# Linear attention: keys times x first, the values' weights applied to that sum

## The chip, the cores and the metric

The kernel runs on one core of a Trainium2 chip. The metric is the device time of a whole execution in microseconds. One execution was also recorded by the hardware profiler; all durations of single instructions come from that execution.

## The reference, cut to what matters

The program is a chain of four layers on x of 2 images, 512 channels and 32 x 32 = 1024 pixels: layer 0 attention with a learned position bias and an MLP, layer 1 a deformable convolution with a gate, layer 2 linear attention, layer 3 softmax attention with 8 heads. The change lies in layer 2:

```python
def delu(x):
    return 10.0 * relu(x) + exp(10.0 * minimum(x, 0.0))
Q = einsum('dc,bcn->bdn', wq, xf) + bq[None, :, None]      # d = 64, c = 512, n = 1024
K = einsum('dc,bcn->bdn', wk, xf) + bk[None, :, None]
V = einsum('ec,bcn->ben', wv, xf) + bv[None, :, None]      # e = 512
Qf = delu(Q).transpose(0, 2, 1)
Kf = delu(K)
KV = einsum('bmn,bcn->bmc', Kf, V)
norm = 1.0 / einsum('bnd,bd->bn', Qf, sum(Kf, axis=-1) + EPS)
attn = einsum('bnd,bdc,bn->bcn', Qf, KV, norm)
return x + gamma[0] * attn
```

KV can be had in two orders. With V made first, it is Kf times V. With Kf times x made first, it is that 64 x 512 sum times wv, plus the sum of Kf over the pixels times bv.

## The kernel before, in words

All data is fp32. x lies in SBUF as `x_all`, with channels on partitions in four blocks (`CC` = 4) and pixels along the free dimension; each layer updates it in place. TensorE executes in exactly the order of the program text (a manual schedule). The instructions of the other engines are ordered by a planner, which mixes the streams of work on each of them; every engine then runs its own list in order. Layers are interleaved by Python generators: a `yield` in one lets the caller advance another.

Layer 1's deformable convolution has three parts for each image. `Products.run` makes, for each of 9 taps k, a table in DRAM: 8 pixel blocks of 128, each of four 128x512 matmuls `py` (L1281), copied by ScalarE to `y` (L1289, four buffers) and written by a DMA on SP's queue. `Samples.gather` fetches rows of that table by indirect DMAs that GpSimd issues (L1333), two for each block, 16 for each tap. `Samples.due` lets a tap's gathers start only when its table is complete. `Samples.add` accumulates what was gathered on VectorE (`dfacc`, L1344). `gate_image` ends the layer for one image.

Layer 2, `Linear.run`, is executed once per image:

- `pqk` (L1430): queries and keys of one half of the pixels in one 128-row result, queries in rows 0 to 63 and keys in rows 64 to 127; VectorE and ScalarE apply `delu`.
- In eight steps t, one per block of 128 pixels: `pv` (L1455), four 128x512 matmuls for the values, which VectorE evicts with the bias to `v` (L1463). At t=1 the keys are transposed (`pk`, L1468) and copied to `kf`. At t=3 the sum of the keys is made (`pks`, L1477). From then on each step also adds kf times v to `pkv` (L1448). At t=5 and t=6 the norms `pn` of the two halves follow (L1494), a reciprocal, and the scaling of the queries.
- `pkv` is copied to `kv` (L1509), and eight matmuls `pa` (L1514) with 64 rows apply it to the queries; VectorE adds each to x (L1522).

For image 0 this runs between the `py` matmuls of image 1's tables, one step of layer 2 for each block of a table, while image 1's gathers are under way. Then come layer 3's normalization `h` (L1612) and its queries and keys (`pq`, L1652) for image 0, with `gate_image` of image 1 among the last of these. For image 1, layer 2 runs together with layer 3's values of image 0 (`Attention.values`, L1629): `weave` takes one matmul of the values after each step of layer 2, and the rest of them (14) at the end. After that layer 3's heads start with scores `pl` (L1719), their maximum on VectorE (L1807), exponentials on ScalarE and transposes `pt` (L1769).

PSUM banks: layer 2 takes its results from a ring of five banks (`bank`) and one bank of its own for `pkv`; tables and values take a ring of two (`turn`).

Of the kernel before, what the change touches and what calls it, by code (L numbers as in the profile page):

```python
# [9 lines left out]
F32 = mybir.dt.float32  # L10
# [96 lines left out]
def layouts(i):  # L107
# [21 lines left out]
    for r in (0, 32, 64, 96):  # L129
        off_b[r : r + 18, 0] = np.asarray(i["L1_conv_off_b"])  # L130
    parts.append(("off_b", off_b))
    parts.append(("bqk", np.concatenate([i["L2_conv_bq"], i["L2_conv_bk"]]).reshape(128, 1)))
    parts.append(("gamma", _column(i["L2_conv_gamma"])))
    for name in ("gn_scale", "gn_bias", "b_out"):
        parts.append((name, _per_partition(i["L3_conv_" + name])))
# [18 lines left out]
    for g in range(8):  # L154
        vw_stack[64 * (g % 2) : 64 * (g % 2) + 64, g // 2] = vw[g].T

    off_w = np.asarray(i["L1_conv_off_w"]).reshape(18, CC, 128, 9).transpose(2, 1, 3, 0)
    dc_w = np.asarray(i["L1_conv_dc_w"]).reshape(C, CC, 128, 9).transpose(2, 3, 1, 0)
    qkv = np.asarray(i["L3_conv_W_qkv"]).reshape(C, 8, 3, 64)
    arrays = {  # L160
        "x": np.asarray(i["x"]).reshape(B, C, HW),
# [13 lines left out]
        "a_pw_w": _rows(np.asarray(i["L1_conv_a_pw_w"]).reshape(C, 256).T),  # L175
        "off_w": off_w,
        "dc_w": dc_w,
        "wqk": _rows(np.concatenate([i["L2_conv_wq"], i["L2_conv_wk"]]).T),
        "wv": _rows(np.asarray(i["L2_conv_wv"]).T),
        "dc_b_row": np.asarray(i["L1_conv_dc_b"]).reshape(1, C),  # L180
        "bv_row": np.asarray(i["L2_conv_bv"]).reshape(1, C),
# [94 lines left out]
def layers(net, out):  # L276
# [11 lines left out]
    with ExitStack() as later:  # L288
# [57 lines left out]
        with ExitStack() as l1:  # L346

            ps_m = net.psum(l1, "l1_m", 5)
            kv_bank = net.bank(l1, "l2_kv")
            banks["turn"] = net.psum(l1, "l1_y", 2)  # L350

            def bank(name):
                return ps_m.tile([128, 512], F32, name=name, tag="bank")

            att = Attention(net, later)
            l2 = ExitStack()
            linear = Linear(net, l2)
            own1 = ExitStack()
            f1 = Features(net, 1, own1)
            more = net.pool(own1, "df_more", 2)  # L360
            sums0.pools += [more, more]
            found = f1.run(bank, True)
            for i, _ in enumerate(made):
                some(found, 2)
                if i % 4 < 3:
                    sums0.due(taken)
            some(found, 99)
            sums1 = Samples(net, f1, products, own1, 1)
            sums1.pools += [more, more]
            tmp = net.pool(own1, "df_tmp", 1)  # L370
            made = products.run(f1, turn)
            taken1 = sums1.run()
            aside = None
            for i, _ in enumerate(made):
                if i == 62:
                    sums1.pools = sums1.pools[:3]
                if aside is None:
                    if next(taken, None) is None:
                        aside = gate_image(net, f0, sums0, tmp, bank)
                        wait = i + 4  # L380
                else:
                    sums1.due(taken1)
                    if i >= wait and next(aside, None) == "gated":
                        own0.close()
                        ctx2 = ExitStack()
                        extra = net.pool(ctx2, "df_extra", 2, side="right")
                        sums1.pools += [extra, extra]
                        linear.open(ctx2, side="right")
                        aside = chain(
                            linear.run(0, bank, kv_bank),  # L390
                            group_norm_terms(net, linear.tmp, 0, bank),
                        )
            for _ in aside:
                next(taken1, None)
            ctx2.close()
            image0.close()

            att.open_first(later, side="right")
            for _ in att.normalize(0):
                next(taken1, None)  # L400
            keys = chain(*(att.queries_keys(0, hp, turn) for hp in range(CC)))
            for i in range(48):
                next(keys)
                if i % 2 == 0:
                    next(taken1, None)
            some(taken1, 99)
            weave(keys, gate_image(net, f1, sums1, tmp, bank))
            own1.close()
            with ExitStack() as ctx:
                att.open_values(later, side="right")  # L410
                linear.open(ctx)
                weave(linear.run(1, bank, kv_bank), att.values(0, turn))
            l2.close()
        layer3(net, att, later, out)

# [2 lines left out]

FOUND = (1, 0, 0, 1, 2, 2, 2, 2, 0, 1, 1, 0, 3, 3, 3)
MADE = 11  # L420


def first_layer(net, pool, feat, p, q):
# [983 lines left out]
class Linear:  # L1407


    def __init__(self, net, ctx, **kw):  # L1410
        self.net, nc = net, net.nc
        w = net.pool(ctx, "l2_w", **kw)
        self.wqk, self.wv = net.load("wqk", w), net.load("wv", w)
        self.bv = net.load_row("bv_row", w)
        self.ones = w.tile([128, 64], F32, name="ones2", tag="ones2")
        nc.gpsimd.memset(self.ones, 1.0)
# [4 lines left out]
    def run(self, b, bank, kv_bank):  # L1421

        net, nc, x, tmp = self.net, self.net.nc, self.net.x, self.tmp
        qk = []
        for n in range(2):
            pqk = bank("pqk")
            for cc in range(CC):
                nc.tensor.matmul(  # L1430
                    pqk,
                    lhsT=self.wqk[:, cc, :],
                    rhs=x[:, b, cc, half(n)],
                    start=(cc == 0),
                    stop=(cc == CC - 1),
                )
            qf = tmp.tile([128, 512], F32, name="qkf", tag="qkf", bufs=2)
            e = tmp.tile([128, 512], F32, name="e2", tag="e2")
            nc.vector.tensor_scalar(qf, pqk, net.vec("bqk"), None, ALU.add)
            delu(nc, qf, e, qf)  # L1440
            qk.append(qf)
            yield
        pkv, pending = None, None
        kf = tmp.tile([128, 8, 64], F32, name="kf", tag="kf")
        norms = []

        def product(t, v):
            nc.tensor.matmul(  # L1448
                pkv[:64, :], lhsT=kf[:, t, :], rhs=v, start=(t == 0), stop=(t == 7)
            )  # L1450

        for t in range(8):
            pv = bank("pv")
            for cc in range(CC):
                nc.tensor.matmul(  # L1455
                    pv,
                    lhsT=x[:, b, cc, 128 * t : 128 * t + 128],
                    rhs=self.wv[:, cc, :],
                    start=(cc == 0),
                    stop=(cc == CC - 1),  # L1460
                )
            v = tmp.tile([128, C], F32, name="v2", tag="v2", bufs=4)
            nc.vector.tensor_tensor(v, pv, self.bv, ALU.add)  # L1463
            if t == 1:
                pk = bank("pk").rearrange("p (t d) -> p t d", d=64)
                for u in range(8):
                    at = 128 * (u % 4)
                    nc.tensor.transpose(  # L1468
                        pk[:, u, :],
                        qk[u // 4][64:128, at : at + 128],  # L1470
                        net.cst("ident", slice(64, 128))[:, 64:128],
                    )
                nc.scalar.copy(kf, pk)
            if t == 3:
                pks = bank("pks")
                for u in range(8):
                    nc.tensor.matmul(  # L1477
                        pks[:64, :64],
                        lhsT=kf[:, u, :],
                        rhs=self.ones,  # L1480
                        start=(u == 0),
                        stop=(u == 7),
                    )
                ksum = tmp.tile([64, 64], F32, name="ksum", tag="ksum")
                nc.vector.tensor_scalar(ksum, pks[:64, :64], 1e-10, None, ALU.add)
                pkv = kv_bank("pkv")
                for part in pending:
                    product(*part)
                pending = []
            if t in (5, 6):  # L1490

                pn = bank("pn")
                qf = qk[t - 5][:64, :]
                nc.tensor.matmul(pn[:64, :], lhsT=ksum, rhs=qf, start=True, stop=True)  # L1494
                norm = tmp.tile([64, 512], F32, name="norm", tag="norm")
                nc.vector.reciprocal(norm, pn[:64, :])
                nc.vector.scalar_tensor_tensor(
                    qf, norm, net.vec("gamma", rows=slice(0, 64)), qf, ALU.mult, ALU.mult
                )
            if t > 3:  # L1500
                for part in pending:
                    product(*part)
                pending = []
            pending = (pending or []) + [(t, v)]
            yield
        for part in pending:
            product(*part)
        kv = tmp.tile([64, C], F32, name="kv", tag="kv")
        nc.scalar.copy(kv, pkv[:64, :])  # L1509
        yield  # L1510
        for n in range(2):
            for oc in range(CC):
                pa = bank("pa")
                nc.tensor.matmul(  # L1514
                    pa,
                    lhsT=kv[:, 128 * oc : 128 * oc + 128],
                    rhs=qk[n][:64, :],
                    start=True,
                    stop=True,
                )  # L1520
                xt = x[:, b, oc, half(n)]
                nc.vector.tensor_tensor(xt, xt, pa, ALU.add)  # L1522
                yield

# [364 lines left out]
```

## Time and profile before

| | |
|---|---|
| median of 3 runs | 4014.14 us (4012.45 to 4018.51) |
| the profiled execution | 4015.97 us |
| its span in the profile | 4014.2 us |
| granted TensorE clock, mean | 0.992 |
| TensorE busy | 3895.0 us (97%) |
| VectorE busy | 2980.4 us (74%) |
| ScalarE busy | 2530.8 us (63%) |
| GpSimd busy | 339.3 us (8%) |
| values matmuls `pv` of layer 2 (L1455) | 128 records, 57.5 us busy |
| table matmuls `py` (L1281) | 1152 records, 515.5 us busy |
| accumulations `dfacc` (L1344) | 560, 409.3 us busy |

The profile's times are microseconds from the span's start; PE is TensorE, PEld its loads of weights, DVE VectorE, ACT ScalarE, POOL GpSimd, SP the engine whose queue carries most DMAs. One fp32 matmul is two records on TensorE, since it makes two passes; a transpose is one. Records of matmuls overlap[...]: busy time on TensorE is therefore more than the sum of the steps from start to start.

### The profile page before, as it was taken

To read this page: it belongs to the slowest core of one execution; us is meant where nothing else is said; L and a number is where in the kernel's file an instruction comes from. 1 tells how busy PE (TensorE), PEld (TensorE's weight loads), DVE (VectorE), ACT (ScalarE), POOL (GpSimd) and SP (SyncE) were. 2 spreads that over 40 slices of the span, in tenths; PEclk is the share of its full clock that TensorE was granted. 3 is DMA by queue.
4 is the path that set the end of the run, shared out by engine and by line. 5 is a ranking of instruction groups with operands and counts; after the bars stand their busy time and mean duration, and the time that the engine had idled before them with its cause. 6 is when DMAs were issued, how large, how long until landed. Compare 5 with 4: busy or idle time off the path is not lost. (4 is left out here: it accounts for less than half of the span.)

```text
span 4014.2 us, 59880 instructions
## 1 busy us (share of the span) xinstructions
PE 3895.0 (97%) x25548; PEld 1499.3 (37%) x25548; DVE 2980.4 (74%) x3326; ACT 2530.8 (63%) x2848; POOL 339.3 (8%) x325
## 2 busy tenths in 40 slices
PE   7999999999999999999997999999999999999999
PEld 4322222222222222222323444444434344355555
DVE  7999999999999999999983104054768677466665
ACT  7999999999999999999991112111112112155544
POOL 0000000000000000000000000033445343000000
PEclk9999999999999999999998999999999999999999
DMA  3000000000000000000002000166779685000000
GB/s 105 8 15 22 22 22 1 22 22 22 22 1 22 22 22 22 1 22 22 1 9 97 0 0 24 36 217 222 271 268 366 233 325 186 0 1 11 1 19 24
DMA packets 90479, 274.39 MB, mean 68 GB/s; under 512 B 9140, under 2 KB 10804, under 8 KB 86884
## 3 DMA queue, kind: packets, MB, share of 16 engines
q0 software_dynamic: 42432, 154.39, 11.0%
q1 hardware_dynamic: 47780, 116.18, 8.0%
q8 instruction: 200, 3.28, 0.3%
q14 instruction: 67, 0.55, 0.0%
HBM read 228.33 MB, written 42.21 MB: 67 GB/s over the span
## 5 line engine op out<-in xcount | busy, mean ns | idle before, releaser
L814 PE MATMUL ph<-h,w_t 128*32 128x512 f32 x16384 | 1796.0, 593 | 15.5 <-ACT lo L824 7.1
L794 DVE TENSOR_TENSOR h<-ab 128x1024 f32<-128x1024 f32 x1024 | 1206.4, 1220 | 73.5 <-PE ph L814 72.5
L814 PEld LDWEIGHTS ph<-h,w_t 128*32 128x32 f32 x16384 | 530.2, 110 | 1255.9 <-issue 1072.8
L803 ACT ACTIVATE h<-h 128x1024 f32<-128x1024 f32 x832 | 870.0, 1065 | 46.2 <-DVE h L794 43.4
L827 DVE SCALAR_TENSOR_TENSOR hi<-lo,low_w,hi 128x1024 f32<-128x1024 f32 x512 | 655.4, 1280 | 30.0 <-ACT hi L826 29.3
L826 ACT ACTIVATE hi<-ph,size_b,size 128x1024 f32<-128x1024 f32 x512 | 620.1, 1211 | 15.3 <-PE ph L814 9.5
L824 ACT ACTIVATE lo<-ph,vec_t 128x1024 f32<-128x1024 f32 x512 | 570.9, 1115 | 2.4 <-PE ph L814 2.4
L1344 DVE SCALAR_TENSOR_TENSOR dfacc<-got,wts,dfacc 128x512 f32<-128x512 f32 x560 | 409.3, 749 | 210.6 <-DMA got<-table,idx 198.2
L1281 PE MATMUL py<-dc_w_t,d 128*128 128x512 f32 x1152 | 515.5, 601 | 21.2 <-ACT y L1289 21.0
L1289 ACT COPY y<-py 128x512 f32<-128x512 f32 x144 | 83.5, 584 | 502.2 <-PE py L1281 424.4
L1333 POOL DMA_INDIRECT got<-table,idx x288 | 318.6, 1106 | 516.3 <-DVE dfacc L1344 157.6
L1281 PEld LDWEIGHTS py<-dc_w_t,d 128*128 128x128 f32 x1152 | 217.4, 192 | 302.0 <-issue 266.6
L1815 ACT ACTIVATE e<-pl,m 128x1024 f32<-128x1024 f32 x128 | 143.5, 1121 | 226.2 <-DVE m L1807 226.2
L1807 DVE TENSOR_REDUCE m<-pl 128x1 f32<-128x1024 f32 x128 | 150.8, 1220 | 144.5 <-PE pl L1719 144.5
L835 PE MATMUL sim<-hi,w 128*32 128x512 f32 x2048 | 244.8, 592 | 1.8 <-DVE hi L827 1.8
L1016 PE MATMUL ph<-xn,mlp_w_t 128*128 128x512 f32 x512 | 229.6, 593 | 0.0
L1005 PE MATMUL acc<-h,mlp_w_t 128*128 128x512 f32 x512 | 229.4, 592 | 0.0
L1024 ACT ACTIVATE h<-ph,vec_t 128x512 f32<-128x512 f32 x64 | 44.0, 687 | 254.2 <-PE ph L1016 254.0
L1069 POOL MEMSET x_pad<- 128x1156 f32 x2 | 2.2, 1094 | 2061.9 <-PE ph L814 2061.9
L1769 PE MATMUL pt<-cst_t,e 128*128 128x128 f32 x1024 | 147.8, 277 | 5.8 <-ACT aT L1780 3.0
L1769 PEld LDWEIGHTS pt<-cst_t,e 128*128 128x128 f32 x1024 | 117.6, 141 | 92.6 <-issue 61.2
L1005 PEld LDWEIGHTS acc<-h,mlp_w_t 128*128 128x128 f32 x512 | 97.3, 190 | 121.9 <-issue 121.6
(228 smaller groups left out, 2536.9 us busy)
## 6 DMA issues: line engine op xcount, KB each, us to landing
table<-y SPq DMA_DIRECT2D x144, 256.0 KB
ab<-feat_d SPq DMA_DIRECT2D x64, 512.0 KB
dc_w_t<-in_dc_w_dram SPq DMA_DIRECT2D x18, 1024.0 KB
mlp_w_t<-in_mlp_w_dram SPq DMA_DIRECT2D x2, 4096.0 KB
got<-table,idx POOLq DMA_INDIRECT x288
w_qkv_t<-in_w_qkv_dram SPq DMA_DIRECT2D x3, 1024.0 KB
out_dram<-x_all SPq DMA_DIRECT2D x12, 256.0 KB
x_all<-in_x_dram SPq DMA_DIRECT2D x4, 512.0 KB
```

The costliest lines, as they stand in the source:

```text
L794: nc.vector.tensor_tensor(h1, at_x[:, k : k + 1, :].to_broadcast([128, 32, 32]), at_y[:, k, :].unsqueeze(2).to_broadcast([128, 32, 32]), A ...
L803: nc.scalar.activation(h1, h1, AF.Relu)
L814: nc.tensor.matmul(ph[32 * t : 32 * t + 32, half(n)], lhsT=w2[:, c0 : c0 + 32], rhs=pair[t // 2][:, half(n)], start=True, stop=True, skip_ ...
L824: nc.scalar.activation(lo, phs[0], AF.Relu, bias=b2_lo)
L826: nc.scalar.activation(hi, phs[1], AF.Relu, bias=size_b, scale=size)
L827: nc.vector.scalar_tensor_tensor(hi, lo, low_w, hi, ALU.mult, ALU.add)
L835: nc.tensor.matmul(sim[32 * t : 32 * t + 32, half(n)], lhsT=w3[:, 30 - j : 62 - j], rhs=sums[t][:, half(n)], start=(j == 0), stop=(j == 30 ...
L1005: nc.tensor.matmul(accs[oc], lhsT=self.w2[:, m, 128 * oc : 128 * oc + 128], rhs=hs[m], start=(m == 0), stop=(m == 15),)
L1281: nc.tensor.matmul(py, lhsT=f.d[:, cc, 128 * c : 128 * c + 128], rhs=w[:, cc, :], start=(cc == 0), stop=(cc == CC - 1),)
L1333: nc.gpsimd.indirect_dma_start(out=g[:, 2 * dy : 2 * dy + 2, :].rearrange("p s c -> p (s c)"), out_offset=None, in_=self.products.tables[f ...
L1344: self.net.nc.vector.scalar_tensor_tensor(acc, g[:, s, :], self.f.wts[:, c, k, s : s + 1], self.f.bias if (k, s) == (0, 0) else acc, ALU.mult,
L1769: nc.tensor.transpose(pt[:, 128 * c : 128 * c + 128], e[:, 128 * k : 128 * k + 128], ident)
```

## The change

Each step t now transposes its block of x (`px`, four 128x128 transposes) and copies it to SBUF (`xt`), on ScalarE for even t and on VectorE for odd t. `pkx` sums keys times x over the eight steps: for each step four matmuls with a 128x128 block of `xt` as weights and 64 columns of `kf`. At the end the 512 x 64 sum is copied twice side by side (`kx`), four 128x512 matmuls with wv make `pkv` in both halves of the rows, and one VectorE instruction adds bv times the key sum (`kv`).

The queries' and keys' weights are stored in both orders, so that the first half of the pixels has its queries in rows 0 to 63 and the second half in rows 64 to 127. The keys' transposes are therefore of whole 128-row blocks, in two groups (t=1 and t=2). The norms of both halves are one step (t=5), on two tiles of the array, with one reciprocal of 128 rows. The products `pa` of the two halves are issued as pairs, one on rows 0 to 63 and one on rows 64 to 127 of the array.

For image 1, a list written by hand says how many values matmuls of layer 3 follow each step; it has 16 entries and adds up to 32, so none is left for the end.

```diff
-    parts.append(("bqk", np.concatenate([i["L2_conv_bq"], i["L2_conv_bk"]]).reshape(128, 1)))
+    bq, bk = (np.asarray(i["L2_conv_" + name]) for name in ("bq", "bk"))
+    parts.append(("bqk", np.stack([np.concatenate([bq, bk]), np.concatenate([bk, bq])], axis=1)))
...
-        "wqk": _rows(np.concatenate([i["L2_conv_wq"], i["L2_conv_wk"]]).T),
+        "wqk": _rows(np.concatenate([wq, wk, wk, wq]).T),
...
-                weave(linear.run(1, bank, kv_bank), att.values(0, turn))
+                values = att.values(0, turn)
+                for i, _ in enumerate(linear.run(1, bank, kv_bank)):
+                    some(values, BESIDE[i])
+                some(values, 99)
...
+BESIDE = (1, 3, 2, 2, 2, 2, 2, 2, 2, 2, 3, 3, 2, 2, 1, 1)
...
-                    lhsT=self.wqk[:, cc, :],
+                    lhsT=self.wqk[:, cc, 128 * n : 128 * n + 128],
...
-        def product(t, v):
-            nc.tensor.matmul(
-                pkv[:64, :], lhsT=kf[:, t, :], rhs=v, start=(t == 0), stop=(t == 7)
-            )
+        queries = [qk[n][64 * n : 64 * n + 64, :] for n in range(2)]
+        kf = tmp.tile([128, 8, 2, 64], F32, name="kf", tag="kf")
+        def product(t, xt):
+            for cc in range(CC):
+                nc.tensor.matmul(
+                    pkx[:, 64 * cc : 64 * cc + 64],
+                    lhsT=xt[:, 128 * cc : 128 * cc + 128],
+                    rhs=kf[:, t, 0, :],
+                    start=(t == 0 and cc == 0),
+                    stop=(t == 7 and cc == CC - 1),
+                    skip_group_check=True,
+                )
         for t in range(8):
-            pv = bank("pv")
+            px = bank("px")
             for cc in range(CC):
-                nc.tensor.matmul(
-                    pv,
-                    lhsT=x[:, b, cc, 128 * t : 128 * t + 128],
-                    rhs=self.wv[:, cc, :],
...
+                nc.tensor.transpose(
+                    px[:, 128 * cc : 128 * cc + 128], x[:, b, cc, 128 * t : 128 * t + 128], ident
+                )
+            xt = tmp.tile([128, C], F32, name="xt2", tag="xt2", bufs=4)
+            if t % 2 == 0:
+                nc.scalar.copy(xt, px)
+            else:
+                nc.vector.tensor_copy(xt, px)
+            if t in (1, 2):
+                n = t - 1
+                pk = bank("pk")
+                for u in range(4):
+                    at = slice(128 * u, 128 * u + 128)
+                    nc.tensor.transpose(pk[:, at], qk[n][:, at], ident)
+                keys = pk.rearrange("p (t v d) -> p t v d", v=2, d=64)[:, :, 1 - n : 2 - n, :]
+                nc.scalar.copy(
+                    kf[:, 4 * n : 4 * n + 4, :, :], keys.to_broadcast([128, 4, 2, 64])
+                )
             if t == 3:
...
+                nc.vector.tensor_copy(ksum, pks[:, :64])
+                nc.vector.tensor_scalar(norms, ksum, 1e-10, None, ALU.add)
+                pkx = kv_bank("pkx")
+            if t == 5:
+                pn = bank("pn")
+                for n in range(2):
+                    r = 64 * n
+                    nc.tensor.matmul(
+                        pn[r : r + 64, :],
+                        lhsT=norms[r : r + 64, :],
+                        rhs=queries[n],
...
+                nc.vector.reciprocal(norm, pn)
+                for n in range(2):
+                    rows = slice(64 * n, 64 * n + 64)
+                    nc.vector.scalar_tensor_tensor(
+                        queries[n], norm[rows, :], net.vec("gamma", rows=rows), queries[n],
+                        ALU.mult, ALU.mult,
+                    )
+            if t > 2:
                 for part in pending:
                     product(*part)
                 pending = []
...
-        nc.scalar.copy(kv, pkv[:64, :])
+        kx = tmp.tile([128, CC, 2, 64], F32, name="kx", tag="kx")
+        nc.scalar.copy(
+            kx,
+            pkx[:, : 64 * CC]
+            .rearrange("p (c d) -> p c d", d=64)
+            .unsqueeze(2)
+            .to_broadcast([128, CC, 2, 64]),
+        )
         yield
+        pkv = bank("pkv")
+        for cc in range(CC):
+            nc.tensor.matmul(
+                pkv,
+                lhsT=kx[:, cc, :, :].rearrange("p v d -> p (v d)"),
+                rhs=self.wv[:, cc, :],
+                start=(cc == 0),
+                stop=(cc == CC - 1),
+            )
+        kv = tmp.tile([128, C], F32, name="kv", tag="kv")
+        nc.vector.scalar_tensor_tensor(kv, self.bv, ksum[:, 0:1], pkv, ALU.mult, ALU.add)
+        yield
+        for oc in range(CC):
+            pas = [bank("pa") for _ in range(2)]
+            for n, pa in enumerate(pas):
                 nc.tensor.matmul(
                     pa,
-                    lhsT=kv[:, 128 * oc : 128 * oc + 128],
-                    rhs=qk[n][:64, :],
+                    lhsT=kv[64 * n : 64 * n + 64, 128 * oc : 128 * oc + 128],
+                    rhs=queries[n],
...
+            for n, pa in enumerate(pas):
                 xt = x[:, b, oc, half(n)]
                 nc.vector.tensor_tensor(xt, xt, pa, ALU.add)
-                yield
+            yield
```

More of the change, by code (lines that the diff above doesn't have):

```diff
@@ L158, in layouts @@
     dc_w = np.asarray(i["L1_conv_dc_w"]).reshape(C, CC, 128, 9).transpose(2, 3, 1, 0)
+    wq, wk = (np.asarray(i["L2_conv_" + name]) for name in ("wq", "wk"))
     qkv = np.asarray(i["L3_conv_W_qkv"]).reshape(C, 8, 3, 64)
@@ L1425, in run @@
         net, nc, x, tmp = self.net, self.net.nc, self.net.x, self.tmp
+        ident = net.cst("ident")
         qk = []
@@ L1438, in run @@
             e = tmp.tile([128, 512], F32, name="e2", tag="e2")
-            nc.vector.tensor_scalar(qf, pqk, net.vec("bqk"), None, ALU.add)
+            nc.vector.tensor_scalar(qf, pqk, net.vec("bqk", n), None, ALU.add)
             delu(nc, qf, e, qf)
@@ L1442, in run @@
             yield
-        pkv, pending = None, None
-        kf = tmp.tile([128, 8, 64], F32, name="kf", tag="kf")
-        norms = []
-        def product(t, v):
-            nc.tensor.matmul(
-                pkv[:64, :], lhsT=kf[:, t, :], rhs=v, start=(t == 0), stop=(t == 7)
-            )
-        for t in range(8):
-            pv = bank("pv")
+        queries = [qk[n][64 * n : 64 * n + 64, :] for n in range(2)]
+        pkx, pending = None, []
+        kf = tmp.tile([128, 8, 2, 64], F32, name="kf", tag="kf")
@@ L1454, in run @@
+        def product(t, xt):
             for cc in range(CC):
                 nc.tensor.matmul(
-                    pv,
-                    lhsT=x[:, b, cc, 128 * t : 128 * t + 128],
-                    rhs=self.wv[:, cc, :],
-                    start=(cc == 0),
-                    stop=(cc == CC - 1),
-                )
[L1462 to L1473, printed above, removed]
+                    pkx[:, 64 * cc : 64 * cc + 64],
[4 more added lines that the diff above has]
+                    skip_group_check=True,
+                )
@@ new lines, in run @@
+        for t in range(8):
+            px = bank("px")
[18 more added lines that the diff above has]
+                )
@@ L1477, in run @@
                     nc.tensor.matmul(
-                        pks[:64, :64],
-                        lhsT=kf[:, u, :],
+                        pks[:, :64],
+                        lhsT=kf[:, u, :, :].rearrange("p v d -> p (v d)"),
                         rhs=self.ones,
@@ L1483, in run @@
                     )
-                ksum = tmp.tile([64, 64], F32, name="ksum", tag="ksum")
-                nc.vector.tensor_scalar(ksum, pks[:64, :64], 1e-10, None, ALU.add)
-                pkv = kv_bank("pkv")
+                ksum, norms = (
+                    tmp.tile([128, 64], F32, name=name, tag=name) for name in ("ksum", "norms")
+                )
[10 more added lines that the diff above has]
+                        rhs=queries[n],
+                        start=True,
+                        stop=True,
+                        skip_group_check=True,
+                    )
+                norm = tmp.tile([128, 512], F32, name="norm", tag="norm")
+                nc.vector.reciprocal(norm, pn)
[6 more added lines that the diff above has]
+            if t > 2:
                 for part in pending:
@@ L1489, in run @@
                 pending = []
[L1490 to L1504, printed above, removed]
+            pending.append((t, xt))
             yield
@@ L1507, in run @@
             product(*part)
-        kv = tmp.tile([64, C], F32, name="kv", tag="kv")
-        nc.scalar.copy(kv, pkv[:64, :])
-        yield
-        for n in range(2):
-            for oc in range(CC):
-                pa = bank("pa")
+        kx = tmp.tile([128, CC, 2, 64], F32, name="kx", tag="kx")
[6 more added lines that the diff above has]
+        )
+        yield
+        pkv = bank("pkv")
[6 more added lines that the diff above has]
+                stop=(cc == CC - 1),
+            )
+        kv = tmp.tile([128, C], F32, name="kv", tag="kv")
[4 more added lines that the diff above has]
+            for n, pa in enumerate(pas):
                 nc.tensor.matmul(
                     pa,
-                    lhsT=kv[:, 128 * oc : 128 * oc + 128],
-                    rhs=qk[n][:64, :],
+                    lhsT=kv[64 * n : 64 * n + 64, 128 * oc : 128 * oc + 128],
+                    rhs=queries[n],
                     start=True,
```

## The prediction

> **What bounds the kernel now.** I read first the page's slices: TensorE is at 9 tenths or more nearly everywhere, so its work counts wherever layer 2 runs. Then busy time by stretch, to find the two stretches with layer 2 in them and the one between:
>
> ```profile
> core 0: us, PE busy (x) PEld busy (x) DVE busy (x) ACT busy (x) POOL busy (x), PEclk, DMA share, GB/s
> 3124.00:3280.00 156.00, 145.97 (x345) 58.60 (x344) 112.42 (x170) 20.75 (x34) 57.78 (x55) 0.99 0.69 253
> 3280.00:3372.00 92.00, 84.69 (x192) 37.13 (x191) 75.69 (x115) 19.01 (x28) 53.94 (x48) 0.96 0.91 331
> ...
> 3398.00:3484.00 86.00, 86.00 (x210) 32.57 (x210) 34.78 (x50) 4.39 (x6) 0.00 (x0) 1.00 0.00 0
> ```
>
> Image 1's layer 2 (3398 to 3484) is TensorE alone: no idle, VectorE at 40%, no DMA. Image 0's is mixed: TensorE has 10 us of holes, DMA idles for a third, and behind it lie 92 us with DMA at 0.91. So each image needs its own argument. For image 1, the chain of waits is nothing but TensorE; steps as long as this cost what their starts are apart, not the 592 ns that one record shows:
>
> ```profile
> 3407.34 3.43 PE pv L1455 x8
> 3410.77 0.86 PE pv L1629 x2
> ...
> 3438.11 1.00 PE pn L1494 x2
> 3439.11 1.00 PE pkv L1448 x2
> 3440.12 1.06 PE pv L1629 x2
> ...
> 3455.21 1.05 PE pa L1514 x2
> ```
>
> One 128x512 matmul is two passes of 0.429 us. A product with 64 rows or columns costs 1.00 to 1.05 instead of 0.86, and the layer 3 matmul after it 1.06. For image 0, GpSimd's timeline shows what the gathers of image 1 wait for (idle time in brackets):
>
> ```profile
> 3201.03 0.94 POOL L1333 DMA_INDIRECT got<-table,idx  x1 [34.54 <-issue]
> ...
> 3247.37 0.94 POOL L1333 DMA_INDIRECT got<-table,idx  x1 [23.96 <-DVE x_all L1522]
> ...
> 3280.78 0.95 POOL L1333 DMA_INDIRECT got<-table,idx  x1 [1.21 <-DMA table<-y]
> ```
>
> These open the batches of taps k=4, 5 and 6 (16 gathers each, counted back from the last). A batch may start when all eight parts of its table are made (matmuls py, L1281) and written: part eight of k=4 ends at 3194.0, of k=5 at 3240.4, of k=6 at 3271.9, 7 to 9 us earlier. So up to 3280 TensorE's progress sets the gathers, whatever the releaser named; from 3280.8 the last 48 gathers run with DMA full, until 3363.
>
> **The change, TensorE's part, for one image.** Removed: pv 8 x 3.43 = 27.4; pk 0.8; pks 1.1; pkv 8 x 1.00; pn 2 x 1.00; pa 8 x 1.05 = 8.4. With pqk (6.9, kept) that is 54.6. Check in image 1: 54.6 + 32 values matmuls x 0.858 = 27.5 + 15 slowed ones x 0.2 = 85.1; between the first pqk and the first pl lie 84.5.
>
> Added, with the nearest rows (the first from line L739's own view, first and last start in it; the others from TensorE's timeline):
>
> ```profile
> L739 PE MATMUL pv<-vw_t,kvbd x16: 222/275/275, 82.3 to 83.9; 128*128 128x64 f32 x16
> ...
> 3383.92 0.60 PE L1379 MATMUL pt<-cst_t,dfacc 128*128 128x128 f32 x4
> 3384.36 1.02 PE L1652 MATMUL pq<-h,w_qkv_t 128*128 128x512 f32 x2
> ...
> 3483.17 1.99 PE L1719 MATMUL pl<-qk 64*128 64x512 f32 x8
> ```
>
> Four transposes hold the array 0.44 us (3383.92 to 3384.36): px 8 x 0.44 = 3.5, pk 2 x 0.44 = 0.9. The product pkx has the 128x128 weights and 64 columns of L739, 15 steps in 1.6 us, 0.107 us a pass: 64 passes = 6.8; pks 16 x 0.107 = 1.7. pkv, now once, 4 x 0.858 = 3.4. L1719 has the form of the new pa: eight passes on two row tiles in four starts 0.43 apart after a first of 0.53. A pair is 0.53 + 0.43 + 0.1 for the switch = 1.06: pa 4 x 1.06 = 4.2, pn 1.06. With pqk: 28.5.
>
> Two rules of the Trainium skill speak against these sums, both on the page "TensorE: Matmul & The Clock Gate". In "The mechanism" of Part 3 it says that a weight load overlaps a running matmul only on other row groups. Then a pkx pass would be its load (128 columns at the 0.84 ns that the loads of 64 and 128 columns differ by, 136 and 190 ns: 0.107) plus its stream (64/512 of 0.429: 0.053), 0.160 us, and pkx plus pks 4.3 us dearer per image. L739 shows 0.107 with just such weights, so I take that and keep 4.3 for the range. In Part 4 it puts a transpose in context at about 275 ns, and says that it does not count as busy for the clock. The trace has 273 ns as a record's length too, but starts 0.11 apart, and layer 3, full of transposes, has a granted clock of 1.00 from 3520 to the end. By the rule px and pk would be 11 us instead of 4.4, the other 6.6 for the range.
>
> **Image 1.** 28.5 + 27.5 + five switches x 0.2 = 57.0 against 84.5: 27.5 less, if nothing waits. Walking through the changed kernel's instruction order with these times, each eviction is ready before its reader: 1.7 us of values matmuls follow each step and three (2.6) stand between the last pkx and pkv and between pkv and pa, where ACT's copy kx (0.58) and DVE's kv (0.75) must pass. The reciprocal (3.35, now once) delays only a values eviction. But behind the first pa stand 8 additions of 0.69, 8 statistics of 0.68, 4 aggregates of 0.2 and 3 evictions of 0.68 on VectorE, 14 us, and layer 3's first maximum queues behind them; TensorE brings its scores 11.3 us after that point. Before, 12 us of values matmuls lay there as cover. So 2.7 come back: **24.8 gained**. The 14 us in themselves are not new.
>
> **Image 0.** Here VectorE's order matters: the copies of odd xt stand behind 6, 12 and 12 more accumulations dfacc (0.67 each), kv behind 10 of k=4's. The even copies (0.58) go to ScalarE behind a y copy. Walked through: the third py still waits till 3140.8 and the fourth till 3147.8 for the y copies queued behind delu's exponentials, so that of the first 6 us saved all but 1.5 are lost; xt of t=1 comes at 3157.5, when TensorE has just done pks; xt of t=3 at 3166.1, a hold of 2 us (before, 4.5 us were lost at 3166 for v); part eight of k=4 ends at 3176.3, **17.7 earlier**. The gathers start 7 us later, at 3183; the tenth accumulation was 15.2 us after that start before, so kv comes at 3199.3 and holds pa by 2.4. Then pa pairs and py alternate: k=5 ends at 3217.6 (22.8 earlier), k=6 at 3247.4 (**24.5 earlier**), with the 2 us at pvar kept. A batch took about 28 us (3201 to 3229), so k=5's, from 3225, is through when k=6's table is written at 3256. From there the full DMA needs its 82 us as before, and the last parts py need 55 as before. Then h, which waits for the last tables, the keys pq and the gate follow unchanged: **24.5 gained**. DMA can take it: in 3124 to 3280 it idled 0.31 x 156 = 48 us.
>
> What else: wqk is 256 KB larger, loaded near 2500, where the slices show hardly any DMA: 0.7 us at 364 GB/s, hidden in the offset convolution, and 0.7 at most if that cover went. VectorE loses 8 additions v and a reciprocal (8.8 us an image) and gets 4 copies of 0.68 and three small ones. POOL's order stays; SP only moves a table write about a weight load. The rest is not touched.
>
> Sum: the profiled execution took 4015.97 us (span 4014.2 and 1.8 around it). 4015.97 - 24.5 - 24.8 = 3966.7. The median of the runs, 4014.14, is 1.8 below that execution: **3965 us**.
>
> **Rivals.** *The gathers keep their pace* (0.14): image 0's gain stays below 8 us, because tables written into a fuller DMA land late and the y buffers (four) stop TensorE. For it: ACT waited 10.6 us for y's buffers around 3260, under a batch. Against it: from 3280 to 3330, with DMA at 0.98, py ran without a hole. Image 1 alone gives 4014.1 - 24.8 = 3989. *Small matmuls pay in full* (0.11): loads unhidden, transposes 275 ns, row tiles one after the other (4.2 + 1): 16 us an image, 3965 + 32 = 3997, or 3974 to 3990 for a part of it. *VectorE's queue holds TensorE* (0.03, slower): xt of t=1, 3, 5 and kv stand behind accumulations that wait for gathers, and these for tables which the held TensorE makes. A batch lasts 28 us, so four holds of half of one are 56, more than the 49.3 gained: 4021. It decides from 12.3 us a hold; the trace has 4.5 and 1.0 for the like, and the accumulations in front of the copies belong to taps before k=4, whose gathers had all been issued by 3166. *The order hides the change* (0.02): image 1 waits on its chain of hand-overs and image 0 on gathers, 4010 or so.
>
> **How the numbers follow.** The likeliest case has 0.70: 3965, and 3955 to 3976 with its own unknowns (image 0 between 16 and 26.5, image 1 between 22 and 27.5, and a few us of the runs' spread, 4012.45 to 4018.51). Up to 3990 the range takes in most of the first two rivals: 3954 to 3990. About 0.2%, 8 us, is what a measurement of this kernel tells from no change. Faster by more than that: 0.95; the same 0.02; slower 0.03.
>
> **What would show it.** Right: batches opening near 3183, 3225 and 3256; the last gather issued near 3338; image 1's first pqk at 3374 instead of 3398.6 and first pl at 3431 instead of 3483; pkx passes 0.107 apart, pa's two row tiles starting together. Wrong: pkx starts 0.16 or more apart; holds over 5 us at pkx or pa on DVE; y copies waiting for DMA between 3225 and 3303; layer 3's first maximum over 5 us after its scores.

## The result, and the profile after

| | before | after |
|---|---|---|
| median of 4 runs each | 4016.32 us (4012.45 to 4022.08) | 3967.93 us (3965.57 to 3970.08) |
| ratio | | 0.9879, 95% interval 0.9864 to 0.9893 |
| span of the profiled execution | 4014.2 us | 3965.4 us |
| granted TensorE clock | 0.992 | 0.989 |
| first pqk of image 0 | 3121.53 | 3122.42 |
| image 0: first pqk to first pqk of image 1 | 277.1 us | 252.5 us |
| of it: tables / wait for h / keys pq | 207.7 / 7.3 / 62.1 | 182.5 / 8.2 / 61.8 |
| image 1: first pqk to first pl | 84.6 us | 58.6 us |
| first pl to the end | 531.0 us | 531.9 us |

The span fell by 48.8 us: 24.6 in image 0's stretch, 26.0 in image 1's, less 0.9 at the entry and 0.9 behind. The last five rows, the stages, are taken from the start times in TensorE's timeline; the experiments below are compared by them too.

Busy time by stretch of the changed kernel, same columns as before (us, busy PE, PEld, DVE, ACT, POOL, granted clock, DMA share, GB/s). The stretches answer to the three of before:

```profile
3122.00:3257.00 135.00, 126.39 (x379) 60.71 (x378) 106.84 (x168) 23.15 (x40) 58.88 (x55) 0.96 0.82 306
3257.00:3349.00 92.00, 83.84 (x191) 36.74 (x190) 75.95 (x116) 18.96 (x28) 54.46 (x48) 0.96 0.88 317
3374.00:3434.00 60.00, 58.91 (x234) 31.24 (x234) 27.90 (x45) 7.23 (x11) 0.00 (x0) 1.00 0.00 1
```

Image 1 (third line) is still TensorE alone, in 60 us instead of 86. In the first line DMA's share rose from 0.69 to 0.82: the same gathers, closer together. But the granted clock is 0.96 there, where it was 0.99. What that costs is worked out in the last section.

The transposes, products and row-tile pairs of image 1, from TensorE's timeline (start, length, engine, line, operation, records); ahead of it the line of all pkx records from L1464's own view:

```profile
L1464 PE MATMUL pkx<-kf,xt x128: 219/275/323, 3157.4 to 3413.3; 128*128 128x64 f32 x128
...
3399.15 0.60 PE L1476 MATMUL px<-cst_t,x_all 128*128 128x128 f32 x4
3399.59 1.00 PE L1464 MATMUL pkx<-kf,xt 128*128 128x64 f32 x8
3400.43 1.94 PE L1680 MATMUL pv<-w_qkv_t,h 128*128 128x512 f32 x4
...
3422.12 1.13 PE L1564 MATMUL pa<-qkf,kv 64*128 64x512 f32 x4
3423.18 1.98 PE L1680 MATMUL pv<-w_qkv_t,h 128*128 128x512 f32 x4
...
3433.46 1.99 PE L1770 MATMUL pl<-qk 64*128 64x512 f32 x8 [1.09 <-DVE x_all L1573]
```

Read the starts, not the lengths. Four transposes take 0.44 us (3399.15 to 3399.59), eight pkx passes 0.84 us (to 3400.43), which is 0.105 a pass although each record is 0.275 us long; a pa pair, four records, takes 1.06 us (3422.12 to 3423.18). The last line is the one hold of image 1: the first scores wait 1.09 us for VectorE's last addition.

GpSimd's timeline, the openings of the batches k=4, 5 and 6, counted back from the last gather:

```profile
3181.53 0.93 POOL L1343 DMA_INDIRECT got<-table,idx  x1 [17.09 <-DVE xt L1483]
...
3222.18 0.94 POOL L1343 DMA_INDIRECT got<-table,idx  x1 [18.71 <-DVE dfacc L1354]
...
3259.26 0.96 POOL L1343 DMA_INDIRECT got<-table,idx  x1 [14.14 <-DMA table<-y]
```

They were 3201.03, 3247.37 and 3280.78. And TensorE's waits between 3117 and 3440 (us in total, times, longest):

```profile
PE pq L1703 <- ACT h L1663: 8.2, 1, 8.2
PE py L1291 <- ACT y L1299: 3.7, 2, 2.5
PE pvar L1605 <- DVE spread L1602: 3.6, 1, 3.6
...
PE pl L1770 <- DVE x_all L1573: 1.1, 1, 1.1
...
PE pa L1564 <- DVE kv L1558: 0.7, 1, 0.7
PE pks L1497 <- DVE xt L1483: 0.4, 1, 0.4
```

### The profile page after: what moved, and what is told of

Its sections match the earlier page's. It is cut to its first block, busy times and chain, and to the rows that moved or that the text cites. A ratio compares the mean times of both kernels' runs of the same rounds, so it can differ in the third digit from the quotient of the medians.

```text
span 3965.4 us, 59982 instructions
## 1 busy us (share of the span) xinstructions
PE 3847.6 (97%) x25596; PEld 1498.6 (38%) x25596; DVE 2967.5 (75%) x3320; ACT 2536.3 (64%) x2858; POOL 340.7 (9%) x325
## 5 line engine op out<-in xcount | busy, mean ns | idle before, releaser
L1291 PE MATMUL py<-dc_w_t,d 128*128 128x512 f32 x1152 | 523.9, 610 | 23.1 <-ACT y L1299 23.1
L1034 ACT ACTIVATE h<-ph,vec_t 128x512 f32<-128x512 f32 x64 | 44.0, 687 | 254.2 <-PE ph L1026 254.0
```

The source lines that it names most:

```text
L1291: nc.tensor.matmul(py, lhsT=f.d[:, cc, 128 * c : 128 * c + 128], rhs=w[:, cc, :], start=(cc == 0), stop=(cc == CC - 1),)
```

## The experiments

e1, e2, e3 and e9 ran on one chip, e4 to e7 on another, e0, e8 and e10 on a third and e11 on a fourth, each group beside runs of the kernel before. Across groups, ratios to before and stages are what can be compared.

**Which image pays, and does the order alone.** In e1 only image 1 has the new order, in e2 only image 0 (`run_values` is the kernel's old `run`, values first); e9 is the kernel before with a list for image 1 that leaves no values matmuls for the end.

```diff
e1:
-                            linear.run(0, bank, kv_bank),
+                            linear.run_values(0, bank, kv_bank),
e2:
-                for i, _ in enumerate(linear.run(1, bank, kv_bank)):
-                    some(values, BESIDE[i])
-                some(values, 99)
+                weave(linear.run_values(1, bank, kv_bank), values)
e9, against the kernel before:
-                weave(linear.run(1, bank, kv_bank), att.values(0, turn))
+                values = att.values(0, turn)
+                for i, _ in enumerate(linear.run(1, bank, kv_bank)):
+                    some(values, BESIDE[i])
+                some(values, 99)
+BESIDE = (1, 3, 2, 2, 2, 2, 2, 2, 2, 2, 4, 1, 1, 1, 1, 1, 1, 1, 1)
```

> Image 0 runs layer 2 in the old order (values first), image 1 in the new one. Theory (TensorE's own work in each image, the two gains simply add): only image 1's 25 us are left, 0.9938 of before, 3991 us beside 4016. Rival (image 0's gain comes from DMA that was idle anyway, and image 1's start is set by the gathers whatever image 0 does): image 1's part would be about all, 3970.

> Image 0 runs layer 2 in the new order, image 1 in the old one with one values matmul of layer 3 after each step. Theory: 24 us are left, 0.994 of before, 3992 us, with the batches of gathers opening near 3182, 3222 and 3259 as in the changed kernel. Rival (the gathers keep their pace): less than 8 us, 4008 or more.

> The kernel before, but image 1's values matmuls of layer 3 follow a list written by hand like the changed kernel's (two after most steps, 8 among the pa) in place of one after each step and 13 at the end. Theory (TensorE was full there, so the order gains nothing): no gain, 0.999 to 1.002 of before, perhaps 2 us slower because the cover at the end is gone. Rival (image 1's gain is the list's): 5 us or more faster, 0.9988 or less.

| | median us | ratio to before (4015.82) | image 0 | image 1 |
|---|---|---|---|---|
| e1, image 1 alone | 3989.92 | 0.9941 (0.9924 to 0.9957) | 272.0 | 58.6 |
| e2, image 0 alone | 3997.98 | 0.9957 (0.9940 to 0.9974) | 254.2 | 84.6 |
| e9, list alone | 4015.16 | 0.9997 (0.9988 to 1.0006) | 276.8 | 84.6 |

Image 1 alone brings its 26.0 us whole, and the list without the new order brings nothing. So the gain is arithmetic taken off TensorE, not a better weave. Image 0's looks softer: in its old order the stretch took 277.1, 276.8 and 272.0 us in three executions, in the new one 252.5 and 254.2. In e2 the keys pq also waited 3.2 us for a ScalarE eviction queued behind the gate's `rstdn`, which waits for the last accumulations; the whole kernel's wait there was 1.0. e2's median is 6 us above what was expected of it, and e1's and e2's savings (25.9 and 17.8) sum to 43.7 instead of 48.4; the intervals are too wide to call that a real difference.

Windows of 1 us show what is the same in every execution. They split the stretch of image 0 into TensorE's idle time, the busy time lost to the clock (busy time times one minus the granted clock), and the rest, which is its work at full clock (worked out from the profile's busy times):

| image 0's stretch | us | idle | lost to the clock | work |
|---|---|---|---|---|
| before | 277.1 | 18.2 | 4.1 | 254.8 |
| e9, old order | 276.8 | 16.4 | 5.1 | 255.2 |
| e1, old order | 272.0 | 13.7 | 3.8 | 254.5 |
| changed | 252.5 | 17.7 | 6.6 | 228.1 |
| e0, changed kernel again | 250.9 | 19.5 | 2.9 | 228.5 |
| e2, new order | 254.2 | 22.1 | 3.8 | 228.3 |

The work is 26 to 28 us less with the new order, about as in image 1 (26.0 and the 1.1 us of the hold at pl), and it repeats within 1 us; the scatter of the stretch is idle time and clock. In seven of the other executions below it lies between 227.5 and 228.3 us; e3 has more.

**The row-tile pairs undone.** The two halves of pa become two steps, each followed by values matmuls, so that they no longer run side by side.

```diff
             for n, pa in enumerate(pas):
+                if n == 1:
+                    yield
                 nc.tensor.matmul(
...
-BESIDE = (1, 3, 2, 2, 2, 2, 2, 2, 2, 2, 3, 3, 2, 2, 1, 1)
+BESIDE = (1, 3, 2, 2, 2, 2, 2, 2, 2, 2, 2, 2, 1, 1, 1, 1, 1, 1, 1, 1)
```

> The changed kernel, but each pa stands alone: a step of other work lies between the two of a pair, in both images (the list of image 1 then has 20 entries with one values matmul after each pa). Theory (two row tiles run side by side, a pair in 1.06 us; alone each costs 1.05 and slows its neighbour by 0.2): 4 x (2 x 1.05 + 0.2 - 1.06) = 5 us an image on TensorE, of which image 1 may get 1 to 2 us back at the start of layer 3, since its statistics are less crowded: 3976 beside 3968. Rival (the pairs gain nothing, all of the gain is in the values): no difference, 3968.

Measured: 3972.31 us, ratio 0.9891 (0.9874 to 0.9907), with image 0 at 258.2 and image 1 at 62.4 instead of 58.6. From e3's TensorE timeline:

```profile
3425.83 1.12 PE L1566 MATMUL pa<-qkf,kv 64*128 64x512 f32 x2
3426.88 1.12 PE L1682 MATMUL pv<-w_qkv_t,h 128*128 128x512 f32 x2
3427.94 1.12 PE L1566 MATMUL pa<-qkf,kv 64*128 64x512 f32 x2
```

One half alone takes 1.05 us, a pair 1.06: the second half is free on the other rows. For image 1 that is four starts of 1.05 and four more values matmuls at 1.06 instead of 0.86, 5.0 us, less the 1.1 us at pl, which is gone here: 3.9, and 3.8 was measured. In image 0, by the same split as above, TensorE's work is 233.0 us instead of 228.1. By the ratios to before (0.9891 against 0.9879) the pairs are worth 0.12%, some 5 us, but the two intervals overlap; the stages are the firmer numbers.

**The list, and who copies xt.** e4 puts one values matmul after each step of image 1 and leaves the rest for the end; e6 and e7 give all eight copies xt to VectorE or to ScalarE.

```diff
e4:
-                for i, _ in enumerate(linear.run(1, bank, kv_bank)):
-                    some(values, BESIDE[i])
-                some(values, 99)
+                weave(linear.run(1, bank, kv_bank), values)
e6 and e7:
-            if t % 2 == 0:
-                nc.scalar.copy(xt, px)
-            else:
-                nc.vector.tensor_copy(xt, px)
+            nc.vector.tensor_copy(xt, px)
or
+            nc.scalar.copy(xt, px)
```

> The changed kernel, but image 1 takes one values matmul after each step of layer 2 and the other 16 at the end, as before. Theory (TensorE's work is the same 57 us, but 0.86 us no longer cover each hand-over between engines): the first pqk to the first pl of layer 3 grows from 58.6 us by the uncovered waits at pk, pkx, pkv and pa, 4 to 8 us, less the 2 us that the 16 matmuls at the end cover: 2 to 6 us slower than the changed kernel. Rival (the list of steps is what gains in image 1): 10 us or more slower.

> The changed kernel with all eight copies xt on VectorE. Theory (copies behind accumulations hold TensorE at pkx): in image 0 the three first pkx wait for the copy of t=2, one more batch of accumulations, 4 to 8 us, and part of it stays in the opening of k=4's gathers: 2 to 6 us slower. Rival (VectorE's queue is not felt): within 1 us.

> The changed kernel with all eight copies xt on ScalarE. Theory (the holds at pkx by VectorE's copies were 0.5 us in all, the y copies behind the exponentials stay): within 1.5 us of the changed kernel, as image 1 may gain a little on VectorE's crowded end. Rival (the odd copies on VectorE still cost image 0 several us): 3 us or more faster.

One run each, the kernel before at 4015.25 on that chip: 3963.27, 3966.74 and 3966.78. Two expectations missed. In e4 nothing waits in image 1; its timeline shows the pairs with one values matmul between them and the rest in one row ahead of pl, which no longer waits:

```profile
3413.79 1.13 PE L1562 MATMUL pa<-qkf,kv 64*128 64x512 f32 x4
3414.85 14.86 PE L1678 MATMUL pv<-w_qkv_t,h 128*128 128x512 f32 x34
3429.64 1.99 PE L1768 MATMUL pl<-qk 64*128 64x512 f32 x8
```

So the hand-overs need less cover than I had given them, and the plain order is 1.0 us shorter for image 1 (57.6). The other miss is e6: the odd copies' danger, VectorE's queue, costs 1.4 us in three waits at pkx, although all eight copies stand in it.

**Do image 1's last gathers set the end of image 0's stretch?** e5 leaves out the 16 gathers and 32 accumulations of the last tap, k=8, of image 1. e11 leaves out only the gathers; the accumulations read the last block gathered for k=7.

```diff
e5:
-        for k in range(9):
+        for k in range(9 - self.f.b):
e11, in gather:
+        if (f.b, k) == (1, 8): return self.last
...
-        g = pool.tile([128, 4, C], F32, name="got", tag="got")
+        g = self.last = pool.tile([128, 4, C], F32, name="got", tag="got")
```

> The changed kernel without the gathers and accumulations of the last tap k=8 of image 1 (the table is still made and written); left out are 16 of its 144 gathers. Theory A, as the prediction put it (from the batch k=6 on the full DMA sets the end): image 1's first pqk comes some 20 us earlier, near 3355. Theory B, from the changed kernel's trace (the way goes over the last py, its table write, h and the keys pq; the gate's data lie ready 8 us before TensorE gets to them): the first pqk comes at most 3 us earlier, by a shorter wait of h for its memory.

> Leaves out the 16 gathers of image 1's last tap (k=8); its 32 accumulations stay and use the last block that was gathered for k=7. Unlike in e5, the normalization h then stands in ScalarE's list ahead of the gate's rstdn, as in the changed kernel. Theory A (image 0's end is set by TensorE's own path, last py, h, keys pq): the first pqk of image 1 comes 250 to 253 us after that of image 0, as in the changed kernel (252.5 and 250.9 in two executions), with some 8 us of h and 61 to 63 us of pq, and the time is within 2 us of the changed kernel's. Theory B (the gathers set it): the first pqk comes 3 us or more earlier, up to the 8 us or so by which the last accumulations end sooner, and the time falls by as much.

e5 took 3975.22 us in its one run (image 0 258.2), e11 3970.56 us, ratio 0.9885 (0.9868 to 0.9901), image 0 258.7. None of the expected outcomes named these numbers. With fewer gathers image 0 ended later, and the traces say why. In e5 the planner put the gate's `rstdn` ahead of h in ScalarE's list, and h waited behind it (the wait for h: 13.8 us instead of 8.2):

```profile
3308.65 0.58 ACT L1299 COPY y<-py 128x512 f32<-128x512 f32 x1 [2.85 <-PE py L1291]
3320.61 0.21 ACT L1377 ACTIVATE rstdn<-rstdn 128x4 f32<-128x4 f32 x1 [11.38 <-DVE rstdn L1376]
3321.09 4.63 ACT L1663 ACTIVATE h<-x_all,add,mul 128x1024 f32<-128x1024 f32 x4 [0.27 <-DMA got<-table,idx]
```

In e11 `rstdn` stands where it did, but VectorE reaches the statistics only after nearly all accumulations, so the eviction behind `rstdn` is late. TensorE's timeline of e11, and below it VectorE's share of the stretch in which no gather is left (windows of e11, same columns as above):

```profile
3313.18 30.36 PE L1703 MATMUL pq<-h,w_qkv_t 128*128 128x512 f32 x64 [7.42 <-ACT h L1663]
3347.61 19.05 PE L1703 MATMUL pq<-h,w_qkv_t 128*128 128x512 f32 x38 [4.07 <-ACT qk L1721]
...
3313.00:3352.00 39.00, 34.75 (x69) 14.82 (x70) 37.23 (x69) 9.20 (x14) 1.82 (x2) 0.85 0.13 47
```

VectorE is busy for 37.2 of 39 us without a gather under way, against 37.5 in the changed kernel, and its last step before the gate ends at 3353.5 instead of 3352.2. So these last gathers set nothing: VectorE's own accumulations end then in either case, 7 to 8 us before 3360.2, when TensorE needs them in the changed kernel. TensorE's work in the stretch is that of the changed kernel, 227.7 us in e5 and 227.5 in e11; what made it longer by 5.7 and 6.3 us is idle time (23.3 and 21.3 us instead of 17.7) and clock (7.2 and 10.0 instead of 6.6). That is worked out from the traces; no kernel here ran without either hold. Nor do these two show that an earlier gather sets nothing: in the changed kernel's trace the start of h is put down to a gather's landing, 6.20 us after the last y copy, in e8's to a table write, 5.53 us after it. About 1 us is at stake there.

**Three banks for the tables.** TensorE waits 3.7 us at py for the y copies. e8 gives the ring `turn` a third PSUM bank and takes one from layer 2's; e10 adds e4's plain order; e0 is the changed kernel again, as the yardstick.

```diff
-            ps_m = net.psum(l1, "l1_m", 5)
+            ps_m = net.psum(l1, "l1_m", 4)
-            banks["turn"] = net.psum(l1, "l1_y", 2)
+            banks["turn"] = net.psum(l1, "l1_y", 3)
```

> The changed kernel once more, as the yardstick for the two beside it: 3968 us, within 3 us, with the first pqk of image 1 252 us after that of image 0 and the first pl 58.6 us later.

> The tables' and values' PSUM ring has three banks instead of two, the ring of layer 2 four instead of five. Theory (the waits of py behind the y copies at 3139 and 3147 cost image 0 their time): the 3.7 us of py waiting for ACT y go, k=4's batch opens 2 to 4 us earlier, and the time is 1 to 4 us below the changed kernel's. Rival (the gathers, or layer 2's ring with a bank less, set image 0's end): the batches open earlier but the first pqk of image 1 does not, or new waits at px, pk or pa take the gain: within 1 us of the changed kernel or slower.

> As e8, and with one values matmul after every step of image 1's layer 2 instead of the list. Theory (the list buys nothing, since one matmul covers each hand-over, and costs the 1.1 us at the first pl): 1 us below e8, image 1 at 57.6 us. Rival (with four banks in layer 2's ring a single values matmul no longer covers the hand-overs): pkv, pa or pks wait for VectorE or ScalarE, image 1 at 60 us or more, and the time 1 to 4 us above e8.

| (before: 4024.05) | median us | ratio to before | image 0 | image 1 |
|---|---|---|---|---|
| e0, changed kernel | 3971.79 (3969.77 to 3975.15) | 0.9881 (0.9861 to 0.9901) | 250.9 | 58.6 |
| e8, three banks | 3968.34 (3968.08 to 3973.36) | 0.9875 (0.9855 to 0.9895) | 253.8 | 58.6 |
| e10, and plain order | 3968.74 (3966.09 to 3972.02) | 0.9874 (0.9855 to 0.9894) | 254.3 | 57.6 |

e0 came 0.8 us above the range it was given, on a chip where the kernel before took 4024 us; its ratio is that of the changed kernel. The medians of e8 and e10 are 3 us lower with runs that overlap; the stages show no gain for the bank, and e8's profiled execution had reached image 0's first pqk 5.6 us earlier than e0's (3121.2 against 3126.7). That entry lies anywhere from 3117.4 to 3126.7 in the kernels with two banks too. The waits of e8 say where it went:

```profile
PE pk L1489 <- DVE qkf L1414: 5.1, 2, 2.6
PE pvar L1605 <- DVE dfacc L1354: 3.0, 1, 3.0
...
PE px L1476 <- DVE xt L1483: 2.0, 1, 2.0
```

The y waits are gone, and TensorE arrives at pk before VectorE has finished delu (5.1 us), then at px before an odd xt is copied out of its bank (2.0), in a ring that has one bank less here. The gathers of k=4 open 62.1 us after the first pqk, in e0 59.0 us after it. So the gap belongs to the chain of VectorE and ScalarE at the start of layer 2 rather than to the tables' banks, which was the rival's outcome; a third bank that is not taken from layer 2 was not run. The plain order's 1.0 us shows in image 1's stage both times (e4, e10), and is too small to be told apart in these medians.

## Why the prediction was right

It said 3965 us and 49.3 us saved; 3967.9 was measured, and the profiled span fell by 48.8. Its mechanism, TensorE's work taken away on TensorE's own path, is what the traces show. By its steps:

- **TensorE's new work.** px 0.44, pkx 0.105 to 0.107 a pass, a pa pair 1.06: each as costed. Of the two rules of the Trainium skill weighed against this (page "TensorE: Matmul & The Clock Gate", Parts 3 and 4), neither price was paid: 0.160 a pass is excluded by eight passes in 0.84 us (the section also names a background weight buffer into which a load is pulled ahead, and that would fit), and transposes at 275 ns each by four in 0.44. Whether transposes count as busy for the clock is not shown: the clock stays 1.00 through image 1's stretch with its 40 transposes, but they come there eight at a time at most, under 1 us, between matmuls. The rival of small matmuls paid in full is out, and e3 excludes its part on row tiles.
- **Image 1: 24.8 forecast, 26.0 measured.** The sum of the steps was 27.5 and came to 27.1. The mis-sized term is what comes back behind VectorE's 14 us at the end: 2.7 forecast, 1.1 measured at pl. One values matmul after each step would have been cover enough (e4).
- **Image 0: 24.5 forecast, 24.6 measured**, from errors that cancel; that it is so close is luck, since two executions of the same kernel differ by 1.6 us in this stretch (e0). k=4 opened at 3181.5 (3183 forecast) and k=5 at 3222.2 (3225): the hold at xt of t=3 did not come (2 forecast) and kv held pa for 0.7 instead of 2.4. Part eight of k=6 ended at 3250.0 (3247.4), and its batch opened at 3259.3 (3256). The step "with the 2 us at pvar kept" is the one that failed: pvar was held 3.6 us, and the clock fell behind it, which cost 2.7 more. The forecast has no term for such a loss; the first wait for y brought another 1.8 (last section).
- **The waits for y** were placed right (the py at 3139.3 and 3146.8 were held, 3.7 us in all), and in e8, where they are gone, waits of 5.1 us for the delu chain stand in their place.
- **The end of image 0.** I gave the gathers from k=6 their "82 us as before" with DMA full. The last one was issued near 3338, as forecast, but e5 and e11 show that the last gathers are not what ends the stretch; the other leg, last py, h and keys pq, did, and it happened to give the same number. The rival of gathers that keep their pace is out: DMA took the same gathers at a share of 0.82, and after 3147 no py of image 1's tables waited for a y copy.
- **The slower side.** The rival in which VectorE's queue holds TensorE needed 12.3 us a hold. The largest at xt and kv was 0.7, and 1.4 in all at pkx with all copies on VectorE (e6).

## What to carry to other kernels

Where one engine has next to no holes, cost a rewrite by the distances between starts of the nearest shapes in the same trace: the record lengths would have priced transposes and 64-column products two and a half times too high. When such a change frees 25 us in a mixed stage, list the hand-overs that were hidden before, and allow for a clock loss of 1.5 to 3 us behind each hold of about 2 us or more. Where several streams end close together, leaving one out reorders the others' lists; look at what moved before reading such a run as a verdict.

## What the hardware showed unexpectedly

A hold of TensorE can cost twice its length, because the granted clock can fall behind it. The hold at pvar can be compared in every execution. A run of 512-column passes of py follows it, 120 to 152 of them, which should take 0.429 us each and 0.16 more, by which the last record outlasts its step. The lines are of e3, e0 and the changed kernel:

```profile
3256.47 0.39 PE L1607 MATMUL pvar<-spread,cst_t 128*128 128x4 f32 x2 [1.83 <-DVE spread L1604]
3256.72 53.44 PE L1291 MATMUL py<-dc_w_t,d 128*128 128x512 f32 x120
...
3240.13 0.39 PE L1605 MATMUL pvar<-spread,cst_t 128*128 128x4 f32 x2 [3.06 <-DVE dfacc L1354]
3240.38 65.48 PE L1291 MATMUL py<-dc_w_t,d 128*128 128x512 f32 x152
...
3236.86 68.08 PE L1291 MATMUL py<-dc_w_t,d 128*128 128x512 f32 x152
```

By 0.429 us a pass, 120 should take 51.6 us and 152 should take 65.4: e3 lost 1.8 us, e0 0.1 and the changed kernel 2.7. All fourteen executions:

| behind pvar the clock | hold at pvar, us | lost, us |
|---|---|---|
| stayed at 1.00 | 1.91 (before), 2.18 (e1), 2.50 (e2), 2.70 (e7), 2.80 (e4), 3.06 (e0) | 0.1 each |
| fell to 0.50 | 1.83 (e3), 2.30 (e9), 2.61 (e5), 2.90 (e10), 2.92 (e11), 3.00 (e8), 3.64 (changed), 3.78 (e6) | 1.8, 1.5, 1.8, 3.1, 1.8, 2.8, 2.7, 1.8 |

The windows of the changed kernel show that clock, in the hold and the 13 us behind it:

```profile
3230.00:3240.00 10.00, 6.36 (x13) 2.89 (x12) 8.68 (x17) 2.13 (x4) 7.87 (x8) 0.76 1.02 404
3240.00:3250.00 10.00, 10.00 (x22) 4.25 (x21) 9.68 (x18) 1.17 (x2) 4.51 (x4) 0.90 1.04 419
```

It is the same at other places of image 0's stretch. The first wait for y in the changed kernel, 2.53 us, was followed by a clock of 0.50, and eight passes took 5.40 us instead of 3.6. The keys pq behind h lost 2.1 us (changed, hold of 8.16) and 2.5 (before, 7.31), behind e11's hold of 4.07 us 2.6, and behind e2's hold of 3.17 us nothing. In this stretch of the fourteen traces every hold of 3.6 us or more lost 1.5 to 3.2 us, and of those between 1.8 and 3.2 us some did and some did not.

"TensorE: Matmul & The Clock Gate" of the Trainium skill states in Part 1 that the clock falls to half after an idle window of about 3.4 us and needs a busy one to return, and that the windows run freely. A fall to half that holds of equal length bring or spare agrees with that; the length does not, since 1.83 us was enough, and the measurement decides. What sets the moment stays open.

These losses also account for the 0.96 in the first stretch after, and for much of what two executions of one kernel differ by: e0's tables took 179.1 us and the first profile's 182.5, and nearly all of these 3.4 us is clock (1.4 us lost against 4.6).
